# One-bank PSUM tiles and first conditioning rows from products in a hyperbolic transformer block

## The chip, the core and the metric

The kernel runs on one core of one Trainium2 chip. Its engines are TensorE (PE, matrix products; "PEld" is its weight load), VectorE (DVE), ScalarE (ACT), GpSimd (POOL) and SyncE (SP), which here issues all DMAs from one queue (SPq). The metric is the device time of one execution in microseconds (us). Three runs of the kernel before took 961.23, 961.72 and 963.40 us, so the median is 961.72. One more execution was profiled; it took 956.23 us, of which the span from first to last instruction is 954.2 us.

## What is computed

The input `x` is 128 sequences of 64 positions with 256 features, `cond` is one row of 256 features per sequence. A transformer block in hyperbolic coordinates runs on it, with six conditioning vectors per sequence (shift, scale and gate, for attention and for the MLP):

```python
ada = t_emb @ w_ada + b_ada
sh_msa, sc_msa, g_msa, sh_mlp, sc_mlp, g_mlp = jnp.split(ada, 6, axis=-1)
residual = x
xm = expmap0(layer_norm(logmap0(x)) * (1 + sc_msa) + sh_msa)
q, k, v = (_to_heads(plin(xm, w, b)) for w, b in ((w_q, b_q), (w_k, b_k), (w_v, b_v)))
qt, kt, vt = logmap0(q), logmap0(k), logmap0(v)          # 16 heads of 16
attn = jax.nn.softmax(einsum(qt, kt) / 4)
out_h = expmap0(einsum(attn, vt))
attn_out = plin(_from_heads(out_h), w_o, b_o)
x = mobius_add(residual, expmap0(g_msa * logmap0(attn_out)))
residual = x
xm = expmap0(layer_norm(logmap0(x)) * (1 + sc_mlp) + sh_mlp)
ff = plin(plin(xm, w_f1, b_f1), w_f2, b_f2)
return x_in + mobius_add(residual, expmap0(g_mlp * logmap0(ff)))
```

`expmap0` and `logmap0` scale a row by a function of its norm, and `plin` is a linear layer between them. The kernel folds most of these scalings into per-row factors, and folds the two MLP weights into one matrix `wm`, made once at the start.

## The kernel before

A tile is 128 partitions, which are two sequences of 64 positions. Four tiles (512 rows) are a quad, two tiles a pair; there are 16 quads and 32 pairs. The quads go through the block in groups: [0], [1,2], [3,4], ... [13,14], [15]. For each group the kernel does the attention of its quads (`attention`, with `attention_pair` for each pair), then the scalars of the Möbius addition (`scalars`, `inner`), then the MLP (`mlp`), and later the last addition and the store (`final`).

**The order is planned.** The Python code does not issue instructions. It records operations in `Plan.add`, each with the engines that may do it, a cost guessed by a formula and a key (the quad's number plus an offset for the kind of step from the table `pl.off`). `Plan.run` then plays the program through with five engines and chooses, whenever an engine is free, the ready operation with the lowest key for which buffers are free. `issue` emits the instructions in that order, and on the chip each engine runs its own list in order. So a change of a cost, a buffer count or an offset can move every instruction. `pl.hold` lets an engine wait a little for a better operation.

**Keep-warm products.** Where the plan finds PE with nothing to do and the share of busy time in the last 2.6 us below `share`, it puts in a 128x128 product of the identity with itself (`warm`, line 1394). Its result is read by nobody.

**PSUM.** The eight banks are four tensors of two banks. An operation asks for a "bank" or a "dbl", two neighbouring banks; class `Banks` hands them out. Three kinds of work use a double bank: the Q and K products of a pair (`qk`), whose squares are taken by one ACT instruction of 128x1024; the scores (`sc`), whose exponentials are two such instructions per pair; and attention times V (`av`), after which one reciprocal (line 505) and one product (`z`, line 483) of 128x512 normalise the heads.

**Conditioning.** At the start, `cond` is transposed and multiplied by `w_ada` in three slices of 512 columns; the bias `b_ada` is loaded as three broadcasts to all 128 partitions and added on DVE. The results are written to DRAM (`ada_d`), and `rows` reads them back for each quad so that each sequence's row stands on its 64 partitions. In `modulated`, DVE multiplies the normalised row by (1 + scale) (the tiles `mda`, `mdm`) and POOL (for quad 0 DVE or POOL) adds the shift (line 486). Quad 0 takes this way too: it waits for the first slice to be written and read back.

**Loads.** SP's queue takes cond, the first slice of `w_ada`, quad 0 of x, the bias, then the Q, K and V weights and biases. The rest of `w_ada` comes behind quad 0's first rows. `load_rest` loads the weights of the output projection and of the MLP once the gate rows are written, and makes `wm`. In `final`, the original x is loaded again (`xr`), POOL adds it (line 486, tile `x`), DVE does the last step (`p`), and a quad is stored by one DMA of 512 KB.

The lines named in profiles are those of helpers: 460 and 483 (`ts`, `tt` on DVE), 486 (`tt` on POOL), 494 (`stt`), 505, 509 (reciprocal, reduce), 519 and 521 (copy on DVE, ACT), 537 (ACT), 552 (products), 559 (transposes), 565 and 570 (DMA). Names without numbers are tile tags.

Of the kernel before, what the change touches and what calls it, by code (L numbers as in the profile page):

```python
# [66 lines left out]
class Buf:  # L67


    def __init__(self, ap, tag, bufs, space):  # L70
        self.ap, self.tag, self.bufs, self.space = ap, tag, bufs, space
        self.psum = space == "psum"
        self.n = {"dbl": 2, "bank": 1}.get(tag)
        self.log = []
        self.users = 0
        self.seq = self.place = None


class Banks:


    def __init__(self, pairs):
        self.pairs = pairs
        self.used, self.rel, self.n = [0] * 8, [k - 8 for k in range(8)], 0

    def place(self, k, n):
        return self.pairs[k // 2] if n == 2 else self.pairs[k // 2][:, 512 * (k % 2) : 512 * (k % 2) + 512]

    def room(self, pairs, single):
        n = [self.used[k] + self.used[k + 1] for k in range(0, 8, 2)]  # L90
        free = n.count(0)
        return pairs <= free and single <= n.count(1) + 2 * (free - pairs)

    def take(self, n):
        if n == 2:
            k = min((k for k in range(0, 8, 2) if not self.used[k] + self.used[k + 1]), key=lambda k: (max(self.rel[k : k + 2]), k))
        else:
            k = min((k for k in range(8) if not self.used[k]), key=lambda k: (-self.used[k ^ 1], self.rel[k], k))
        for i in range(k, k + n):
            self.used[i] = 1  # L100
        return k

    def give(self, k, n):
        for i in range(k, k + n):
            self.n += 1
            self.used[i], self.rel[i] = 0, self.n
# [6 lines left out]
class Plan:  # L113
# [3 lines left out]
    def __init__(self, nc, tc):  # L117
        self.nc, self.tc = nc, tc
        self.ops, self.byname, self.tags = [], {}, {}
        self.key, self.st, self.off = 0, "", {}  # L120

        self.early, self.late = 3, 13
        self.hold = {}

        self.span_, self.share, self.fill_occ = 2.6, 0.93, 0.22
        self.filler, self.fill = None, (0.0, 0.0)
        self.open = None
        self.pattern, self.sizes, self.places = None, {}, {}
# [21 lines left out]
    def allocate(self):  # L150

        for tag, (pool, n, bufs) in self.sizes.items():
            if tag == "bank":
                continue
            if tag == "dbl":
                self.banks = Banks([pool.tile([128, n], F32, tag=f"ps_{k}", name=f"ps_{k}", bufs=1) for k in range(bufs)])
                continue
# [5 lines left out]
    def real(self, ap):  # L163
# [7 lines left out]
        return bass.AP(place.tensor, int(place.offset) + p * full + at, [[full, dims[0][1]]] + dims[1:])  # L171

    def region(self, ap):
# [11 lines left out]
        return b, p0, p0 + dims[0][1], lo, hi  # L185
# [59 lines left out]
    def run(self):  # L245
# [3 lines left out]
        left = {}  # L249
# [33 lines left out]
        banks = self.banks  # L283

        def room(o):
            need = [0, 0, 0]
            for b in o.bufs:
                if b in started:
                    continue
                if b.psum:  # L290
                    need[b.n] += 1
                elif b.tag[0] == "j":
# [4 lines left out]
            return banks.room(need[2], need[1])  # L297

        while done < len(ops):
            progress = False  # L300
            for e in engines:
# [27 lines left out]
                if pick is None:  # L329
                    if e == "PE" and self.fill[0] < now < self.fill[1] and banks.room(0, 1):  # L330
# [8 lines left out]
                        o.place = banks.take(1)  # L339
                        o.eng, o.fn, o.occ, o.start, o.bufs, o.key = e, None, self.fill_occ, now, [], (-1, 0)  # L340
                        o.fn = lambda place=banks.place(o.place, 1): self.filler(place)
# [22 lines left out]
                for b in o.bufs:  # L364
                    if b not in started:
                        started.add(b)
                        if b.psum:
                            b.at = banks.take(b.n)
                            b.place = banks.place(b.at, b.n)
                            continue  # L370
# [32 lines left out]
            while events and events[0][0] <= now + 1e-9:  # L403
                _, _, kind, o = heapq.heappop(events)
                if kind:
                    if kind == 2:
                        banks.give(o.place, 1)
                    continue
# [5 lines left out]
                for b in o.bufs:  # L414
                    left[b] -= 1
                    if not left[b] and b.psum:
                        banks.give(b.at, b.n)
                    elif not left[b]:
# [122 lines left out]
    def mm(self, out, lhsT, rhs, start, stop, onto=False):  # L541
# [4 lines left out]
        elif k == 64:  # L546
            occ = 0.031
        elif k <= 4:
# [29 lines left out]
def kernel(  # L578
# [64 lines left out]
        "<": 3.13, "ada": 8.08, "ada<": 8.91, "ada>": 2.63, "adm": 6.68, "adm<": 0.86, "adm>": 3.73, "av": 6.27,  # L643
        "av<": 6.19, "av>": 9, "bx": 3.75, "bx<": 8.35, "bx>": 3.23, "by": 1.72, "by<": 7.27, "by>": 2.51,
        "bz": 8.84, "bz<": 9, "bz>": 8.09, "ch": 1.2, "ch<": 3.12, "ch>": 5.74, "ex": -2.28, "ex<": -1.01,
        "ex>": -2.07, "fya": 0.9, "fya<": -1.8, "fya>": -3.41, "fym": -0.66, "fym<": 0.44, "fym>": -3.06,
        "ga": 0.79, "ga<": 4.18, "ga>": 0.94, "gm": 7.6, "gm<": 6.4, "gm>": 4.08, "hc": -2.34, "hc<": -1.77,
        "hc>": 2.83, "hm": 0.09, "hm<": -1.26, "hm>": 8.38, "hmb": 4.87, "hmb<": 4.58, "hmb>": 3.29, "hw": 8.6,
        "hw<": 6.78, "hw>": 5.72, "hwb": -4, "hwb<": -0.68, "hwb>": 3.2, "kT": -3.99, "kT<": -2.26, "kT>": 7.07,
        "lx": 9, "lx>": 3.17, "mda": -3.73, "mda<": 6.71, "mda>": 2.67, "mdm": 3.44, "mdm<": 3.01, "mdm>": 3.8,  # L650
        "moa": 0.09, "moa<": -3.74, "moa>": 6.19, "mom>": 4.6, "mua": -3.27, "mua<": 8.51, "mua>": 4.6,
        "mum": 5.08, "mum<": -3.98, "mum>": 3.13, "n1": 7.39, "n1<": 7.97, "n2": 1.05, "n2<": -1.65, "n2>": -4,
        "nh": 1.09, "nh<": -3.36, "nh>": -0.28, "pga": -2.31, "pga<": 8.53, "pga>": 8.18, "pgm": 4.91,
        "pgm<": 2.12, "pgm>": 1.51, "qkb": -3.27, "qkb<": -1.57, "qkb>": 3.82, "qkv": 9, "qkv<": 1.92,
        "qkv>": 6.12, "qx": 3.05, "qx<": -3.07, "qx>": 7.2, "rTa": -3.91, "rTa<": -3.14, "rTa>": 5.83,
        "rTh<": 3.67, "rTh>": 0.63, "rTm": -0.86, "rTm<": 2.9, "rTm>": -2.04, "re": 0.52, "re<": -2.11,
        "re>": -2.61, "sc": 1.18, "sc<": -1.46, "sc>": 5.38, "sq": 0.11, "sq<": 5.18, "sq>": 3.43, "sua": -0.37,
        "sua<": 7.36, "sua>": -0.72, "sum": 4.1, "sum<": -1.33, "sum>": 8.02, "tpa": 2.48, "tpa<": 3.09,
        "tpa>": -4, "tpm": -0.56, "tpm<": 4.86, "tpm>": -3.52, "tq": 6.77, "tq<": 4.87, "tq>": 7.82,
        "tz": -1.39, "tz<": 3.93, "tz>": 1.94, "us": -1.51, "us<": 0.46, "us>": 4.29, "ve": -3.97, "ve<": 0.26,  # L660
        "ve>": 5.46, "wm<": 8.02, "wp": 1.64, "wp<": -4, "wp>": 4.46, "x1": 5.15, "x1<": -2.37, "x1>": -0.94,
        "xr": 7.25, "xr<": 5.99, "xr>": -1.89, "xsa": 3.1, "xsa<": -2.4, "xsa>": 2.48, "xsm": 8.6, "xsm<": 9,
        "xsm>": 8.95, "yTa": -1.74, "yTa<": -3.96, "yTa>": -1.77, "yTm": 7.78, "yTm<": -3.37, "yTm>": 8.19,
        "yya": 6.71, "yya<": -3.67, "yya>": -0.48, "yym": 5.91, "yym<": 5.07, "yym>": 4.92, "z": -2.23, "z<": 9,
        "z>": 1.15, "zT": 0.4, "zT<": -0.93, "zT>": 5.34,
# [13 lines left out]

    def dbl(name):  # L680
        return pl.tile(ps, [P, 1024], "dbl", name, 4, space="psum")
# [170 lines left out]

    cond_sb = T([P, D], "z", "cond_sb", 1)
    pl.dma(cond_sb, cond, 128 * KB)

    wada, bada, ada, behind = [], [], [], []
# [5 lines left out]
    wada.append([T([P, 1024], "yTm", f"wada1{c}", 2) for c in range(2)])  # L862
    bada += pair_of("bada0", "x1", 6)
    (ada0, ada1), (bada_, ada_) = pair_of("ada0", "x1", 6), pair_of("bada2", "x1", 6)
    bada.append(bada_)
    ada += [ada0, ada1, ada_]
    for c in range(2):
        pl.dma(wada[0][c], w_ada[c * P : (c + 1) * P, 0:512], 256 * KB)
    load_x(0)
    pl.dma(bada[0], b_ada[0:512].partition_broadcast(P), 256 * KB)  # L870
# [16 lines left out]
    pl.dmas(  # L887
        [
            (bqkv[p : p + 1, c * D : (c + 1) * D], b.unsqueeze(0))
            for p, c, b in ((0, 0, b_q), (0, 1, b_k), (33, 0, b_q), (33, 1, b_k), (64, 0, b_v), (65, 1, b_v))  # L890
        ],
        6 * KB,
    )
    for c in range(2):
        behind.append(pl.dma(wada[1][c], w_ada[c * P : (c + 1) * P, 512 : 6 * D], 512 * KB))
    for n in (1, 2):
        behind.append(pl.dma(bada[n], b_ada[n * 512 : (n + 1) * 512].partition_broadcast(P), 256 * KB))

# [10 lines left out]
    for n in range(3):  # L909
        aps = bank(f"aps{n}")  # L910
        with pl.group("PE"):
            for c in range(2):
                w = wada[0][c] if n == 0 else wada[1][c][:, (n - 1) * 512 : n * 512]
                pl.mm(aps, condT[:, c, :], w, c == 0, c == 1)
        for h in range(2):
            k = 2 * n + h
            part = slice(h * D, (h + 1) * D)
            one = 1.0 if k in (1, 4) else 0.0
            pl.stt(ada[n][:, part], aps[:, part], one, bada[n][:, part], ALU.add, ALU.add)
            if k in (1, 2, 4, 5):  # L920
                k0 = k - 1 if k in (1, 4) else k
                lo = max(0, k0 - 2 * n) * D
                if k in (1, 2, 5):
                    wrote = pl.dma(parts[k0], ada[n][:, lo : (h + 1) * D], (k - k0 + 1) * 128 * KB)
                else:
                    pl.dma(parts[3][:, 0:D], ada[1][:, D : 2 * D], 128 * KB)
                    pl.dma(parts[3][:, D : 2 * D], ada[2][:, 0:D], 128 * KB)

    def load_rest():
# [567 lines left out]
```

## Time and profile before

| | |
|---|---|
| median of 3 runs | 961.72 us |
| profiled execution / its span | 956.23 / 954.2 us |
| mean granted PE clock | 0.905 |
| real products and transposes / keep-warm products in the program | 4769 / 331 |
| bytes moved by DMA | 90.44 MB, 95 GB/s over the span |
| quad 0: first QKV product starts | 24.2 us |
| quad 0: last MLP product ends | 177.6 us |
| last attention product ends | 864.6 us |
| last MLP product of the last quad ends | 931.9 us |

A product in float32 is two passes on PE, a transpose one, and the profile counts passes. A row of the groups reads: line, engine, operation, output tile and inputs, shape, count, then busy us in all and mean ns of one, then the idle time of the engine just before and what ended it. "PEclk" is the clock that PE was granted in each of 40 slices, in tenths. Windows give, for a stretch of the span, the busy time of each engine with the number of instructions in brackets.

### The profile page before, as it was taken

The page shows a single profiled execution, that of the slowest core. Times are in us where ns is not written, and L with a number is a line of the kernel's source. Part 1 is how long each engine was busy: PE and PEld are TensorE (multiplying, and loading weights), DVE is VectorE, ACT ScalarE, POOL GpSimd, SP SyncE. Part 2 cuts the span into 40 slices and gives each one's busy share as a digit, 9 for nine tenths or more (in the row PEclk, how much of TensorE's full clock was granted, in tenths as well). Part 3 has the DMA queues.
Part 4 walks back from the last instruction along what each step waited for, and adds up shares of the span by engine and source line. Part 5 has one row for each costly group of instructions (what it writes and reads, how often), then busy time and mean ns, then how long its engine had stood idle before and what let it go on. Part 6 is the DMA issues. An engine that isn't in the chain of part 4 may idle for free. (4 is left out here: it accounts for less than half of the span.)

```text
span 954.2 us, 24232 instructions
## 1 busy us (share of the span) xinstructions
PE 822.7 (86%) x9334; PEld 582.5 (61%) x9334; DVE 680.8 (71%) x2781; ACT 501.0 (53%) x1482; POOL 123.7 (13%) x100
## 2 busy tenths in 40 slices
PE   7889898998888888888888888888888798787988
PEld 6465555565665675665665666666655575466777
DVE  5668876788846876678764887678755876568964
ACT  2255753467554584456635575465634654355452
POOL 0011200012100121013200221001400221011111
PEclk9989997999998898979898899979979979779989
DMA  7675562324311362115511163114621223113212
GB/s 227 173 222 143 137 140 58 90 68 138 96 36 34 90 175 71 34 36 147 153 45 46 56 189 100 35 35 135 160 50 44 79 79 90 30 39 100 67 55 90
DMA packets 75743, 90.44 MB, mean 95 GB/s; under 512 B 7270, under 2 KB 57708, under 8 KB 75628
## 3 DMA queue, kind: packets, MB, share of 16 engines
q1 hardware_dynamic: 75628, 88.90, 33.8%
q8 instruction: 73, 1.20, 0.5%
q14 instruction: 42, 0.34, 0.1%
HBM read 79.70 MB, written 9.18 MB: 93 GB/s over the span
## 5 line engine op out<-in xcount | busy, mean ns | idle before, releaser
L552 PE MATMUL ps<-wqkv,yTa 128*128 128x512 f32 (+1 forms) x512 | 198.5, 537 | 3.2 <-ACT ja L537 1.0
L552 PEld LDWEIGHTS ps<-wqkv,yTa 128*128 128x128 f32 x512 | 102.8, 210 | 89.1 <-issue 68.6
L552 PE MATMUL ps<-wm,yTm 128*128 128x256 f32 (+1 forms) x512 | 123.9, 400 | 14.2 <-DVE jd L494 2.2
L1394 PE MATMUL ps<-ident 128*128 128x128 f32 x662 | 104.0, 312 | 33.2 <-ACT pt L537 9.6
L552 PEld LDWEIGHTS ps<-wm,yTm 128*128 128x128 f32 x512 | 99.8, 217 | 42.5 <-ACT rTm L521 4.7
L1394 PEld LDWEIGHTS ps<-ident 128*128 128x128 f32 x662 | 92.8, 219 | 47.1 <-ACT pt L537 10.5
L486 POOL TENSOR_TENSOR x<-x,xr 128x512 f32<-128x512 f32 x32 | 41.1, 1302 | 484.2 <-ACT x L537 461.4
L552 PEld LDWEIGHTS ps<-ve,pt 64*64 64x64 f32 x4096 | 72.8, 152 | 10.8 <-issue 5.4
L552 PE MATMUL ps<-ve,pt 64*64 64x17 f32 x4096 | 76.2, 219 | 0.9 <-issue 0.6
L537 ACT ACTIVATE pt<-ps 128x1024 f32<-128x1024 f32 x64 | 61.9, 1019 | 19.8 <-PE ps L552 19.5
L486 POOL TENSOR_TENSOR ya<-ya,mda 128x512 f32<-128x512 f32 x30 | 39.9, 1334 | 201.0 <-ACT p L521 67.1
L552 PE MATMUL ps<-wo,zT 128*128 128x256 f32 x256 | 61.2, 381 | 0.2
L494 DVE SCALAR_TENSOR_TENSOR p<-ps,fh,gm 128x256 f32<-128x256 f32 x64 | 28.7, 479 | 43.9 <-PE ps L552 17.8
L486 POOL TENSOR_TENSOR ym<-ym,mdm 128x512 f32<-128x512 f32 x32 | 42.0, 1316 | 137.4 <-DVE ym L483 78.5
L537 ACT ACTIVATE qx<-ps,par 128x512 f32<-128x512 f32 x64 | 42.7, 684 | 30.8 <-PE ps L552 18.0
L559 PE MATMUL ps<-ident,u 128*128 128x128 f32 x256 | 43.4, 314 | 8.9 <-ACT pt L537 3.4
L537 ACT ACTIVATE ja<-ps,fh 128x256 f32<-128x256 f32 x64 | 30.3, 473 | 36.9 <-PE ps L552 16.2
L552 PEld LDWEIGHTS ps<-wo,zT 128*128 128x128 f32 x256 | 45.9, 190 | 6.1 <-DVE zT L519 1.2
L552 PE MATMUL ps<-qx,kT 32*64 32x128 f32 x2048 | 45.1, 307 | 4.8 <-DVE kT L519 1.2
L552 PE MATMUL ps<-bqkv,rTa 2*128 2x512 f32 x192 | 46.5, 676 | 3.1 <-ACT rTa L521 1.4
L494 DVE SCALAR_TENSOR_TENSOR jd<-ps,ym 128x256 f32<-128x256 f32 x64 | 27.1, 423 | 27.4 <-PE ps L552 23.3
L552 PEld LDWEIGHTS ps<-qx,kT 32*64 32x64 f32 x2048 | 35.4, 145 | 17.2 <-issue 7.7
(274 smaller groups left out, 1535.1 us busy)
## 6 DMA issues: line engine op xcount, KB each, us to landing
mda<-ada_d SPq DMA_DIRECT2D x64, 256.0 KB, 4.3
mdm<-ada_d SPq DMA_DIRECT2D x64, 256.0 KB, 5.0
x<-in_x_dram SPq DMA_DIRECT2D x16, 512.0 KB, 7.0
xr<-in_x_dram SPq DMA_DIRECT2D x32, 256.0 KB, 4.9
ga<-ada_d SPq DMA_DIRECT2D x64, 128.0 KB, 3.1
gm<-ada_d SPq DMA_DIRECT2D x64, 128.0 KB, 3.0
out_dram<-p SPq DMA_DIRECT2D x16, 512.0 KB, 3.9
xp<-in_x_dram SPq DMA_DIRECT2D x26, 256.0 KB, 2.8
```

Of the source, the lines that this page charges most:

```text
L486: fn2 = lambda: self.nc.gpsimd.tensor_tensor(R(out), R(a), R(b), op)
L494: fn = lambda: self.nc.vector.scalar_tensor_tensor(R(out), R(a), R(s), R(b), op0, op1, **({} if accum is None else {"accum_out": R(accum)}))
L537: fn = lambda: self.nc.scalar.activation(R(out), R(a), func, scale=R(scale), **{k: R(v) for k, v in kw.items()})
L552: fn = lambda: self.nc.tensor.matmul(R(out), lhsT=R(lhsT), rhs=R(rhs), start=start, stop=stop, skip_group_check=onto)
L559: fn = lambda: self.nc.tensor.matmul(R(out), lhsT=R(a), rhs=ident, start=start, stop=True, is_transpose=True, skip_group_check=not start)
L1394: nc.tensor.matmul(place[:, 0:P], lhsT=ident, rhs=ident, start=True, stop=True)
```

## The change

It has six parts.

1. **PSUM**: eight tensors of one bank, handed out in turn; `Banks` and `dbl` are gone. Squares of Q and K are two ACT instructions of 128x512 per pair instead of one of 128x1024, exponentials four instead of two, reciprocal and normalisation two each (128x16 and 128x256) instead of one.
2. **First rows from products**: for quad 0 and attention only, the rows of shift and scale are made in PSUM by products. A repeated `cond` (`crep`, 64 columns per sequence) times the first slice of `w_ada`, onto a one-row product that puts in the bias. DVE then does (scale + 1) times the row and adds the shift, straight from PSUM.
3. **Bias of the conditioning** by a one-row product too, from one loaded row instead of 128.
4. **Loads**: quad 0 of x first, then cond, four rows of bias, the first slice of `w_ada`, the Q, K, V weights; in `load_rest` the MLP weights first, then the projection's, then the other slices of `w_ada`, with the two later conditioning products recorded after them. The `xr` loads wait for the MLP of their own quad (`then`) instead of an early row.
5. **The end**: for the last quad the addition of `xr` may go to DVE, and the store is two DMAs of 256 KB. The shift of the conditioning goes to POOL alone up to the third last quad, and to DVE or POOL after that.
6. **The plan's numbers**: `pl.off` has other values throughout, `share` is 0.92 for 0.93, PE's and DVE's `hold` 0.41 and 0.06 for 0.22 and 0.03.

```diff
-        qk = dbl(f"qk{tag}").rearrange("p (t n) -> p t n", t=2)
+        qk = [bank(f"qk{t}{tag}") for t in range(2)]
...
-        pl.act(usq, qk, AF.Square)
+        for t in range(2):
+            pl.act(usq[:, t], qk[t], AF.Square)
...
-        for k in range(2):
+        for k in range(4):
             pl.act(
-                pt[:, 2 * k : 2 * k + 2].rearrange("p r t f e s -> p (r t f e s)"),
-                sc[k].rearrange("p r t f n -> p (r t f n)"), AF.Exp, scale=GC * GC / math.sqrt(HD),
+                pt[:, k].rearrange("p t f e s -> p (t f e s)"), sc[k].rearrange("p t f n -> p (t f n)"),
+                AF.Exp, scale=GC * GC / math.sqrt(HD),
             )
...
-        pl.recip(rd, ah[:, :, :, HD : HD + 1])
-        pl.tt(
-            z.rearrange("p b t h d -> p b (t h) d"), ah[:, :, :, 0:HD], rd.to_broadcast([P, 2, 16, HD]), ALU.mult
-        )
+        for b in range(2):
+            ah = av[b].rearrange("p (h e) -> p h e", h=16)
+            pl.recip(rd[:, b], ah[:, :, HD : HD + 1])
+            pl.tt(
+                z[:, b].rearrange("p t h d -> p (t h) d"), ah[:, :, 0:HD], rd[:, b].to_broadcast([P, 16, HD]), ALU.mult
+            )
...
+    crep = T([P, 2, 8, S], "qx", "crep", 1)
+    pl.copy(crep, condT[:, :, 0:8].unsqueeze(3).to_broadcast([P, 2, 8, S]))
+    conditioning(0)
+    pl.st = "md"
+    first = [bank(f"md{t}") for t in range(4)]
+    with pl.group("PE"):
+        for t in range(4):
+            pl.mm(first[t], onesP[32 * t : 32 * t + 1, :], bada[0][32 * t : 32 * t + 1, :], True, False)
+    for t in range(4):
+        with pl.group("PE"):
+            for c in range(2):
+                pl.mm(
+                    first[t], crep[:, c, 2 * t : 2 * t + 2, :].rearrange("p e s -> p (e s)"), wada[0][c], False, c == 1
+                )
...
+        for t in range(4 if i0 == k0 == 0 else 0):
+            pl.st = "mu" + tag[0]
+            pl.stt(y[:, t, :], first[t][:, D : 2 * D], 1.0, y[:, t, :], ALU.add, ALU.mult)
+            pl.tt(y[:, t, :], y[:, t, :], first[t][:, 0:D], ALU.add)
...
+                last = quads[-1] == NQ - 1
+                pl.tt(x1[:, t - 1 : t + 1, :], x1[:, t - 1 : t + 1, :], xr, ALU.add, eng="DVE/POOL" if last else "POOL")
...
+                if last:
+                    pl.dma(out_t[:, i0 + t - 1 : i0 + t + 1, :], p2[:, t - 1 : t + 1, :], 256 * KB)
...
-    pl.hold = {"PE": (0.22, 9999.0), "DVE": (0.03, 60.0)}
+    pl.hold = {"PE": (0.41, 9999.0), "DVE": (0.06, 60.0)}
```

In the built programs this gives 4784 real products for 4769 and 271 keep-warm products for 331, ACT 96 more instructions for squares and exponentials, DVE 64 more for reciprocals and normalisation, and four DMAs of 256 KB fewer for the rows.

## The prediction

> **What bounds the kernel now.** I read the engine totals first, then the rate by slices, then the same split by stage, then the keep-warm products alone.
>
> ```profile
> PE 822.7 (86%) x9334; PEld 582.5 (61%) x9334; DVE 680.8 (71%) x2781; ACT 501.0 (53%) x1482; POOL 123.7 (13%) x100
> ...
> PEclk9989997999998898979898899979979979779989
> DMA  7675562324311362115511163114621223113212
> ```
>
> PE leads, but 104 of its 822.7 us are the products of line 1394, which compute nothing. Real work is 718.7 us, 75% of the span; no engine is full. A planned, fixed order with short waits on ACT and DVE bounds it, and only the start (DMA row: 7) leans on DMA. Cut at the first QKV product, the end of quad 0's MLP products and the end of the last attention products:
>
> ```profile
> 0.00:24.20 24.20, 18.10 (x121) 14.98 (x121) 13.89 (x59) 6.62 (x20) 0.70 (x6) 1.00 0.74 229
> 24.20:177.60 153.40, 137.97 (x1630) 88.31 (x1628) 113.02 (x478) 72.56 (x199) 13.71 (x10) 0.94 0.56 144
> 177.60:864.60 687.00, 590.55 (x7103) 414.34 (x7101) 489.09 (x1909) 382.36 (x1120) 93.88 (x72) 0.89 0.29 81
> 864.60:954.20 89.60, 76.12 (x491) 64.89 (x487) 64.78 (x336) 39.49 (x143) 15.44 (x12) 0.94 0.27 77
> ```
>
> Columns: stretch and length, then busy us of PE, weight loads, DVE, ACT, POOL, granted clock, DMA share, GB/s. The keep-warm products alone (PE, weight loads, clock, DMA):
>
> ```profile
> 0.00:24.20 24.20, 12.93 (x106) 12.77 (x106) 1.00 0.74 229
> 24.20:177.60 153.40, 5.97 (x26) 5.01 (x24) 0.94 0.56 144
> 177.60:864.60 687.00, 40.36 (x215) 33.41 (x215) 0.89 0.29 81
> 864.60:931.90 67.30, 25.63 (x169) 23.26 (x169) 0.95 0.28 78
> 931.90:954.20 22.30, 19.12 (x150) 18.36 (x150) 0.92 0.23 75
> ```
>
> Each is recorded as two passes. They fill the start and the end; in the middle they are a symptom of gaps of the plan.
>
> **Part by part.** My sum is an identity for PE: span = work + keep-warm + idle, stretch by stretch. The built order of both kernels gives the number of keep-warm products: up to the end of quad 0's MLP 65 before and 4 after; then to the last attention product 107 and 74; then to the last MLP product 84 and 94; behind it 75 and 99. Together 331 and 271.
>
> *Start, to 24.2 us.* What ends the wait here is not the conditioning's way through DRAM: DVE stood only 0.7 us for the loaded rows of line 486's tile. The chain is x's load (landed 7.82), its statistics (8.9 us on DVE and ACT, to 16.72), modulation, transposes. After, x is first in SP's queue: 512 KB ahead of cond's 128 KB. Cond landed 2.2 us after its issue; 384 KB more at 229 GB/s is 1.7, so x lands near 4.7 instead of 7.82, and the chain with two DVE steps put in (a 1024-wide copy, some 1.1, and two at 0.42) ends near 15.5. But the first rows now come from products: eight of 128x512, 16 passes at 0.457 (six passes of the wm stage took 2.74) = 7.3, plus seven one-row bias products, 14 passes at the bqkv row's 0.24 or, four of them side by side, some 2.9. They need wada0, behind x and cond: 1.16 MB, landing near 7.3. The four row biases can run before that; then come the conditioning product (four passes, 1.8, and a bias 0.5) and the eight: 9.6 us, the first of them cold (the first four such passes took 3.78 instead of 1.83), so to about 19. The last row's two DVE steps (0.84) and transposes and copies as before (21.53 to 24.20, 2.7) give the first QKV product near 22.5, **-1.7**. The 10.2 us of new PE work take the place of 50 keep-warm products (12.2 us). Bounds: -4 (all PE work warm) to +2 (wada0 late). SP's queue: x's next three quads and w1 go past the q/k/v biases, which then land near 30; they are needed after eleven us of QKV products for both pairs, at 33, so covered. Two xr loads (0.5 MB at 21.62 us) go behind the start.
>
> *24.2 to 177.6.* Keep-warm 12 to 1, and w1's transposes and wm's products fill in: at 5.97/13 = 0.46 each, **-5.4** (0 to -8; three broadcast biases and four row loads gone are 1.75 MB, 7.7 us of DMA at 229 GB/s, which ends a wait only where a load is late).
>
> *Middle.* 33 fewer keep-warm products at 40.36/107.5 = 0.375: -12.4. Against it stand the split operations:
>
> ```profile
> L537 ACT ACTIVATE pt<-ps 128x1024 f32<-128x1024 f32 x64 | 61.9, 1019 | 19.8 <-PE ps L552 19.5
> L537 ACT ACTIVATE usq<-ps 128x1024 f32<-128x1024 f32 x32 | 32.5, 1017 | 24.6 <-PE ps L552 24.6
> L537 ACT ACTIVATE vsq<-ps 128x512 f32<-128x512 f32 x32 | 19.0, 594 | 32.2 <-PE ps L552 29.8 <-DVE fim L460 1.1 <-DVE kT L519 1.0
> ```
>
> A two-bank step costs 1.02, a one-bank step 0.594. Exponentials: 4 x 0.594 - 2 x 1.019 = 0.34 a pair; squares 2 x 0.594 - 1.017 = 0.17. On DVE 128x256 from PSUM takes 0.418 (x<-ps,ga): 2 x 0.418 - 0.683 = 0.15 for z; a 128x16 reciprocal isn't in the trace: between 128x8 (0.20) and 128x32 (0.349), about 0.25, so 0.15 more. Together 0.81 a pair, 25.9 us over 32 pairs. How much shows? In the chain of waits after 733 us, with six pairs, stand one of six squares, three of twelve exponentials and two and a half of six z steps: 0.03 + 0.085 + 0.125 = 0.24 a pair, 7.6 in all. Bounds 0 and 25.9. I take **-12.4 + 7.6 = -4.8**. The Trainium skill (Advanced Engine Details and Errata, The Read-Write Bubble) speaks against this part: each ACT or DVE instruction shows its memory latency anew, and one instruction may read several banks. Its table in VectorE: DVE Perf Modes gives 172 cycles fixed on ACT's 1.2 GHz, an estimated 0.143 a split and 13.8 us for 96 splits; the rows give 0.17 and 16.4. Either is hidden except where the chain goes through it, so I keep the rows.
>
> Fewer keep-warm products may cool PE. The skill's rule (TensorE: Matmul & The Clock Gate, What's actually happening) is that half clock comes after a whole idle window of some 3.4 us. The trace:
>
> ```profile
> 280.00:284.00 4.00, 2.15 (x11) 1.59 (x12) 1.65 (x6) 1.89 (x7) 0.00 (x0) 1.00 0.38 131
> 284.00:288.00 4.00, 4.00 (x128) 3.24 (x130) 2.04 (x7) 3.07 (x13) 0.00 (x0) 0.63 0.04 9
> 288.00:292.00 4.00, 4.00 (x18) 2.23 (x15) 0.00 (x0) 0.41 (x2) 0.00 (x0) 0.52 0.20 63
> ```
>
> Here 1.85 us idle in four brought 6.8 us at half clock ((0.37 + 0.48) x 4 / 0.5), while PE was full of 64x17 products. By the rule the removal is free; by the row a half-idle stretch does it, and each costs 3.4 us of passes. Mean clock 0.905 means 181 us, some 27 such stretches. I take no change in their number, as gaps shrink too.
>
> *End.* Before: 159 keep-warm products in 44.75 us (0.281 each), 31.4 us of work, 13.5 idle. After: 193 at 0.281 = 54.3 + 31.4 = 85.7 if idle vanishes (-3.9), 99.2 if it stays (+9.6). The order groups the last three MLPs and leaves their final steps (12 x 0.42 on ACT, 5 x 1.30 on POOL, 12 x 0.50 on DVE) behind them. The end itself:
>
> ```profile
> SPq L1493 <- DMA out_dram<-p: 2.6, 1, 2.6
> SPq L1493 <- PE ps L1394: 1.9, 1, 1.9
> ```
>
> After the last output landed the program still waited 1.9 us for keep-warm products. So halving that output and giving one add to DVE (0.7 for 1.3) saves nothing as long as 99 of them stand at the end. Ninety-nine at 19.12/75 = 0.255 are 25.2 for 19.1: I take **+5.0**.
>
> **Sum:** -1.7 - 5.4 - 4.8 + 5.0 = -6.9. The profiled execution took 956.23 (span 954.2 and 2.0 around it), so 949.3. The median shown is 961.72, 5.5 above that execution; with the same step: **954.8**. The eight one-bank tiles, the removed pair allocator and the pauses allowed to the planner act only through this order.
>
> **Rivals.**
> - *Splits exposed* (slower). Every pair's chain usq, reciprocal, exponentials, z is serial, and ACT's waits on PE (24.6 + 19.5 us above) say it sits behind PE. If all 25.9 shows: -6.9 + 18.3 = +11.4, 973.1. It turns slower once 14.5 of the 25.9 is exposed. Against: ACT is at 53%.
> - *Cooler PE* (slower). Five more half-clock stretches: +17.0 - 6.9 = +10.1, 971.8; two even the sum out.
> - *The start's gain goes through* and the end stays: -1.7 - 8.0 - 4.8 + 0 = -14.5, 947.2. For: DMA share 0.74 and 0.56. Against: the end has more keep-warm products.
> - *The order doesn't do what it counts*: gaps return as waits, 961.7.
>
> **Chances.** Forecast 0.36, splits exposed 0.22, cooler PE 0.14, gain goes through 0.19, nothing 0.09. Under 0.2% (1.9 us) either way can't be told from no change; faster 0.52, same 0.11, slower 0.37. All lower bounds together give -28, all upper ones +25; I cut to 942 to 975. The forecast's own range is 949 to 961.
>
> **What would show it.** Right: first QKV product near 22.5; quad 0's MLP products end near 170; 542 keep-warm passes near 85 us; ACT busy near 518; the clock within 0.01 of 0.905; the tail behind the last MLP product 27. Wrong: PE idle in the middle above its 96 us by more than 10; mean clock under 0.89; a QKV product waiting for a bias or for w1.

## The result and the profile after

Four runs of the changed kernel took 790.22 to 792.59 us, median 792.12, beside 962.56 for the kernel before in the same session. The ratio is **0.821** [0.816, 0.826]. I had forecast 954.8 with a range of 942 to 975. Direction right, size wrong by 163 us, which is far outside the range. The times here are medians of all executions; the ratios compare means without the slow executions, those over 1.5% above their kernel's fastest.

The engine totals, the granted clock and the DMA share of the changed kernel:

```profile
span 790.8 us, 24161 instructions
...
PE 738.0 (93%) x9244; PEld 525.5 (66%) x9244; DVE 682.3 (86%) x2842; ACT 502.9 (64%) x1588; POOL 123.5 (16%) x98
...
PEclk9999899999999999999999999998999998999999
DMA  5938436411651157214731364213641225113314
```

DVE and ACT do what they did before (680.8 and 501.0 us then). PE is 84.7 us less busy and 78.7 us less idle (52.8 for 131.5), and its mean clock is 0.976 for 0.905. The same stretches as in the prediction, in the order length, then busy PE, weight loads, DVE, ACT, POOL, clock, DMA share, GB/s:

```profile
0.00:21.90 21.90, 16.21 (x46) 7.01 (x46) 14.08 (x63) 6.23 (x19) 0.70 (x6) 1.00 0.62 204
21.90:166.60 144.70, 138.74 (x1634) 88.47 (x1632) 123.18 (x544) 76.66 (x237) 13.00 (x10) 0.95 0.54 148
166.60:704.00 537.40, 504.84 (x7019) 361.66 (x7020) 471.11 (x1883) 376.48 (x1184) 90.80 (x68) 0.98 0.37 102
704.00:765.90 61.90, 56.27 (x358) 46.86 (x358) 53.60 (x267) 33.51 (x118) 12.19 (x9) 0.97 0.31 86
765.90:790.80 24.90, 21.92 (x194) 21.53 (x192) 20.37 (x89) 10.00 (x32) 6.78 (x5) 1.00 0.34 106
```

| stretch | before | after | difference | my step |
|---|---|---|---|---|
| to the first QKV product | 24.2 | 21.9 | -2.3 | -1.7 |
| to the end of quad 0's MLP | 153.4 | 144.7 | -8.7 | -5.4 |
| to the last attention product | 687.0 | 537.4 | **-149.6** | **-4.8** |
| the end | 89.6 | 86.8 | -2.8 | +5.0 |

So 150 of 163 us lie in the middle, where the change has nothing but the split operations, the tensors, another order and later `xr` loads. There PE idles 32.6 us instead of 96.5, and its keep-warm products take 27.3 us instead of 40.4:

```profile
166.60:704.00 537.40, 27.33 (x152) 22.55 (x152) 0.98 0.37 102
```

Real products take 477.5 us (504.84 - 27.33) instead of 550.2 (590.55 - 40.36). The clock alone, 0.89 to 0.98, would make about 500 of the 550, an estimate.

**What the stall is.** In the prediction I showed the row of `vsq`, the squares of V, with "29.8 <-PE ps L552" as the idle time before it, and used only its duration. One of these waits in the kernel before, in the timeline (start, us, engine, line, operation; in brackets the idle time before it and who ended it):

```profile
370.59 1.02 ACT L537 ACTIVATE usq<-ps 128x1024 f32<-128x1024 f32 x1 [0.43 <-PE ps L552]
...
372.37 4.77 PEld L552 LDWEIGHTS ps<-wm,yTm 128*128 128x128 f32 x15 [1.50 <-issue]
372.38 5.01 PE L552 MATMUL ps<-wm,yTm 128*128 128x256 f32 x14
375.34 0.60 ACT L537 ACTIVATE vsq<-ps 128x512 f32<-128x512 f32 x1 [3.73 <-PE ps L552]
375.97 0.69 DVE L509 TENSOR_REDUCE hs<-vsq 128x32 f32<-128x512 f32 x1 [2.99 <-ACT vsq L537]
```

The pair's QKV products end near 372.4. ACT is free from 371.61. But `vsq` starts at 375.34, in the middle of MLP products that it doesn't read, and DVE stands idle for 2.99 us until it has `vsq` for the sum `hs`. In the built program, the PE instruction whose count this `vsq` waits for is a `wm,yTm` product into columns 384 to 511 of the tensor `ps_2`; `vsq` reads columns 512 to 1023 of the same tensor, which is the other bank. In these programs a wait is placed per tensor, so two banks with unrelated work wait for each other. I counted such waits in the built programs (both instructions touch the same PSUM tensor, no common bank and no common data elsewhere): **518 in the kernel before, none in the changed one**. The waits run in both directions: ACT for PE 112, PE for ACT 108, DVE for PE 101, PE for DVE 79, the rest between ACT and DVE. In the changed kernel's trace no idle time stands before any of the 32 `vsq`, and nobody waits for them (both lists are empty):

```profile
L492 ACT ACTIVATE vsq<-bank x32: 575/605/659, 36.4 to 666.4; 128x512 f32<-128x512 f32 x32
its engine sat idle before it (us, times) until:
who waited for it (us, times):
```

That is a theory with a count; whether the count makes the time is for the runs.

### The profile page after: what moved, and what is told of

Its sections match the earlier page's. It is cut to its first block, busy times and chain, and to the rows that moved or that the text cites. A ratio compares the mean times of both kernels' runs of the same rounds, so it can differ in the third digit from the quotient of the medians.

```text
span 790.8 us, 24161 instructions
## 1 busy us (share of the span) xinstructions
PE 738.0 (93%) x9244; PEld 525.5 (66%) x9244; DVE 682.3 (86%) x2842; ACT 502.9 (64%) x1588; POOL 123.5 (16%) x98
## 4 chain that ended last, share of the span: by engine, by line
DVE 43%; PE 35%; ACT 8%; DMA 7%; issue 4%; SPq 1%; POOL 1%; DVEq 0%; ACTq 0%; POOLq 0%
PE bank L509 25%; PE bank L516 6%; ACT ja L492 5%; DVE jd L449 4%; DVE x L449 4%; PE bank L1373 4%; DMA mdm<-ada_d 3%; DVE hs L464 3%; DVE u L438 3%; DMA xp<-in_x_dram 2%; DVE p L449 2%; DVE ve L438 1%; DVE z L438 1%; DVE mxq L438 1%; DVE ym L438 1%
## 5 line engine op out<-in xcount | busy, mean ns | idle before, releaser
L509 PE MATMUL bank<-wqkv,yTa 128*128 128x512 f32 (+1 forms) x512 | 175.4, 490 | 3.2 <-DVE yTm L474 3.2
L509 PEld LDWEIGHTS bank<-wqkv,yTa 128*128 128x128 f32 x512 | 93.9, 190 | 73.9 <-issue 63.8
L509 PE MATMUL bank<-wm,yTm 128*128 128x256 f32 (+1 forms) x512 | 106.8, 362 | 0.5 <-DVE rTh L474 0.4
L509 PEld LDWEIGHTS bank<-wm,yTm 128*128 128x128 f32 x512 | 89.6, 195 | 17.1 <-issue 2.3
L441 POOL TENSOR_TENSOR x<-x,xr 128x512 f32<-128x512 f32 x31 | 40.4, 1314 | 339.1 <-ACT x L492 326.7
L1373 PE MATMUL bank<-ident 128*128 128x128 f32 x542 | 75.3, 291 | 5.2 <-ACT ja L492 3.7
L1373 PEld LDWEIGHTS bank<-ident 128*128 128x128 f32 x542 | 69.1, 202 | 10.3 <-ACT ja L492 4.0
L492 ACT ACTIVATE pt<-bank 128x512 f32<-128x512 f32 x128 | 67.3, 604 | 10.3 <-PE bank L509 10.2
L509 PEld LDWEIGHTS bank<-ve,pt 64*64 64x64 f32 x4096 | 63.3, 135 | 11.4 <-issue 3.7
L509 PE MATMUL bank<-ve,pt 64*64 64x17 f32 x4096 | 66.7, 208 | 1.0 <-issue 0.9
L509 PE MATMUL bank<-wo,zT 128*128 128x256 f32 x256 | 61.2, 381 | 0.4 <-issue 0.3
L492 ACT ACTIVATE qx<-bank,par 128x512 f32<-128x512 f32 x64 | 43.1, 688 | 13.8 <-PE bank L516 13.8
L516 PEld LDWEIGHTS bank<-ident,u 128*128 128x128 f32 x256 | 30.4, 149 | 22.5 <-ACT pt L492 12.9
L492 ACT ACTIVATE usq<-bank 128x512 f32<-128x512 f32 x64 | 35.4, 596 | 12.1 <-PE bank L509 11.7
```

The lines of the kernel that those rows point to most:

```text
L441: fn2 = lambda: self.nc.gpsimd.tensor_tensor(R(out), R(a), R(b), op)
L492: fn = lambda: self.nc.scalar.activation(R(out), R(a), func, scale=R(scale), **{k: R(v) for k, v in kw.items()})
L509: fn = lambda: self.nc.tensor.matmul(R(out), lhsT=R(lhsT), rhs=R(rhs), start=start, stop=stop, skip_group_check=onto)
L516: fn = lambda: self.nc.tensor.matmul(R(out), lhsT=R(a), rhs=ident, start=start, stop=True, is_transpose=True, skip_group_check=not start)
L1373: nc.tensor.matmul(place[:, 0:P], lhsT=ident, rhs=ident, start=True, stop=True)
```

## The experiments

The rival to "separate tensors" was that the new plan (order, splits, first rows, loads) makes the gain, and that the tensors only come with it. Times are medians; each ratio is against the kernel before on the same chip (957.94 us in the first session, 961.75 in the second, 958.54 in the third; these lie within 0.5% of each other). The plan's model doesn't know of these extra waits, so putting banks into common tensors leaves the recorded order as it is.

**1. The changed kernel, its banks laid as halves of four two-bank tensors.**

```diff
...
         for tag, (pool, n, bufs) in self.sizes.items():
+            if tag == "bank":
+                pairs = [pool.tile([128, 1024], F32, tag=f"bank_{k}", name=f"bank_{k}", bufs=1) for k in range(4)]
+                self.places[tag] = collections.deque(p[:, 512 * h : 512 * h + 512] for p in pairs for h in range(2))
+                continue
```

> The changed kernel with its order kept to the instruction; only the eight banks are the halves of four tensors of two banks, as in the kernel before. In the built program 670 waits then name an instruction that touches only the other bank of the same tensor (0 in the changed kernel, 518 in the one before). Theory 'shared tensor': these waits are what cost the 163 us; the time goes back most of the way, to 900-1000, PE idle rises from 53 us to over 110 and the clock falls under 0.93. Rival 'plan' (the order, the first rows and the loads are the gain): 792 give or take 8, PE idle 50-60.

Measured: **937.43 us**, ratio 0.978 [0.972, 0.985], with 670 waits on the other half. Its totals and clock:

```profile
PE 811.4 (87%) x9244; PEld 561.8 (60%) x9244; DVE 685.2 (73%) x2842; ACT 506.5 (54%) x1588; POOL 124.1 (13%) x98
...
PEclk9999988998999899998799998979998688898999
```

The same instructions on each engine in the same order as in the 792 us kernel, and 145 us of the gain are gone. PE is idle for 122.5 us (933.9 - 811.4) at a clock of 0.921, all as the theory had it.

**2. The kernel before in its own order, with eight tensors.** A two-bank operation is emitted as two.

```diff
-self.banks = Banks([pool.tile([128, n], F32, tag=f"ps_{k}", name=f"ps_{k}", bufs=1) for k in range(bufs)])
+self.banks = Banks([pool.tile([128, 512], F32, tag=f"ps_{k}", name=f"ps_{k}", bufs=1) for k in range(2 * bufs)])
...
+    def emitted(self, fns):
+        (e, _, occ, lat, lock), = self.ops[-1].ways
+        self.ops[-1].ways = [(e, lambda: [f() for f in fns], occ, lat, lock)]
...
         pl.act(usq, qk, AF.Square)
...
+        real = pl.real
+        pl.emitted([lambda t=t: nc.scalar.activation(real(usq[:, t]), real(qk[:, t]), AF.Square, scale=1.0) for t in range(2)])
```

(The exponentials, the reciprocal and `z` likewise.)

> The kernel before with its order kept; its eight banks are eight tensors, and each two-bank instruction is emitted as two one-bank ones in the same place (96 more on ACT, 64 more on DVE, which are 16 and 10 us busy). 'Shared tensor': 800-850, PE idle under 80, clock over 0.95. 'Plan': 960-985, as the added instructions cost and nothing is gained.

Measured: **796.07 us**, ratio 0.831 [0.826, 0.837], 4 us below the theory's interval, no such wait left. Its totals and clock:

```profile
PE 744.7 (94%) x9334; PEld 536.7 (67%) x9334; DVE 680.3 (86%) x2845; ACT 502.2 (63%) x1578; POOL 125.3 (16%) x100
...
PEclk9999999899999999999989999999999989999999
```

The old order, with the old first rows, loads and table, has nearly the whole gain. The intervals of this ratio and of the changed kernel's just touch, so what all the rest is worth together is about 1% and not resolved.

**3. The same, but with the halves of two-bank tensors**: splits without separation.

```diff
+halves = [pool.tile([128, n], F32, tag=f"ps_{k}", name=f"ps_{k}", bufs=1) for k in range(bufs)]
+self.banks = Banks([t[:, 512 * h : 512 * h + 512] for t in halves for h in range(2)])
```

> As the run before, the same split instructions, but on halves of four two-bank tensors; 715 waits on the other bank. 'Shared tensor': no gain, 960-1010. Second rival 'two-bank instructions' (one instruction over two banks holds both until its end, and splitting it sets them free earlier): as fast as the run with eight tensors, 800-850.

Measured: 961.43 us, ratio 1.0038 [1.0005, 1.0070], 715 waits. Splitting costs 0.4%, some 3.6 us, with the 197 further waits that come with it, and brings nothing. Runs 2 and 3 differ in the tensors alone: 165 us.

**4. Only two of eight banks share a tensor** (changed kernel).

```diff
+            if tag == "bank":
+                pair = pool.tile([128, 1024], F32, tag="bank_p", name="bank_p", bufs=1)
+                alone = [pool.tile([128, 512], F32, tag=f"bank_{k}", name=f"bank_{k}", bufs=1) for k in range(6)]
+                self.places[tag] = collections.deque([pair[:, 0:512], pair[:, 512:1024]] + alone)
+                continue
```

> The changed kernel in its own order, with two of its eight banks laid in one two-bank tensor and the other six in tensors of their own: 187 waits in the built program are for an instruction of the other half of the pair, against 0 with eight tensors and 670 with four pairs. Theory (each such wait costs, wherever it falls): a share of 187/670 of the 145 us that lie between eight tensors (792.1 us) and four pairs (937.4 us), so near 792 + 40 = 832 us, 815 to 850, and clock near 0.96. Rival (the loss comes only when most banks are coupled and TensorE cools; one pair is covered by the other six banks): 790 to 800 us at a clock above 0.97.

Measured: **826.47 us**, ratio 0.861 [0.855, 0.868]. The time is the theory's (832), the clock of 0.975 the rival's. One pair costs 34 us:

```profile
PE 750.5 (91%) x9244; PEld 527.7 (64%) x9244; DVE 682.9 (83%) x2842; ACT 504.4 (61%) x1588; POOL 125.1 (15%) x98
...
PEclk9999899999999999999999999999999799999999
```

PE's idle time is 73.6 us for 52.8, at a mean clock of 0.975 for 0.976. So the wait costs by itself, before the clock falls; with four pairs the clock falls too (0.921). PE is also 12.5 us longer busy (750.5 for 738.0) at the same clock, and why is open.

**5. Other halves: banks k and k+4 of the rotation in one tensor.**

```diff
...
+                self.places[tag] = collections.deque(p[:, 512 * h : 512 * h + 512] for h in range(2) for p in pairs)
...
```

> The changed kernel in its own order on four two-bank tensors, as the earlier run with pairs of neighbours (937.4 us), but with banks k and k+4 of the rotation as the two halves, so that the other half is usually the bank of another, older or much younger, operation. In the built program 658 waits still name an instruction of the other half (670 with neighbours). Theory (such a wait costs because its two halves are in use at the same time by unrelated work, whatever their distance in the rotation): 900 to 960 us at a clock below 0.94. Rival (only neighbours hurt, since their products follow each other at once; far halves are long done when they are waited for): 790 to 850 us. The result also tells whether a mere other numbering of the banks would have done the work of eight tensors.

Measured: **961.09 us**, ratio 1.0001 [0.9962, 1.0040]; 1 us above the theory's interval, and the rival is out. The whole gain of 170 us is gone, with the changed kernel's order, splits, first rows and loads all in place. Its profiled execution (span 965.5, one of the three longest of ten):

```profile
PE 824.7 (85%) x9244; PEld 567.3 (59%) x9244; DVE 684.4 (71%) x2842; ACT 507.2 (53%) x1588; POOL 124.2 (13%) x98
```

These are close to the kernel before's totals (822.7, 680.8, 501.0). This numbering of banks is no substitute for separate tensors; others were not tried. Three rows of the waits, first in the changed kernel, then here (who waited and for whom; us in all, times, longest):

```profile
ACT pt L492 <- PE bank L509: 10.2, 7, 3.0
DVE hs L464 <- ACT usq L492: 5.7, 2, 3.9
DVE rd L460 <- PE bank L509: 7.2, 11, 2.1
...
ACT pt L496 <- PE bank L513: 31.9, 18, 6.0
DVE hs L468 <- ACT usq L496: 25.9, 11, 4.0
DVE rd L464 <- PE bank L513: 21.8, 12, 4.2
```

`vsq`, the example above, waits for PE only 2.9 us here and 7.3 us in run 1: the loss sits in other rows than in the kernel before, and no single row prices it. Nor does the count: 518 such waits go with 162 us (the kernel before and run 2), 658 with 170 us and 670 with 145 us. So it may be luck that the share 187/670 came near in run 4. Why far halves are worse than neighbours is open; it may be that neighbours are often taken by the same step. The 20 us that run 1 keeps against the kernel before are therefore not the worth of the rest of the change.

**6. No keep-warm products at all** (they feed nothing, so the output is the same).

```diff
-                o.fn()
+                if o.key != (-1, 0):
+                    o.fn()
```

> The changed kernel without any of its keep-warm products; nothing else is moved. The profile of the changed kernel has 75.3 us of them and 52.8 us of idle TensorE. Theory (the clock stays up because TensorE no longer waits at the shared tensors; keep-warm products fill what is left and some of them are in the way): clock 0.95 to 0.98 and 785 to 800 us. Rival (the clock of 0.976 is bought with the keep-warm products, and the gain of the change rests on them): clock below 0.93, PE busy on real products up by 30 us or more, 815 us or longer.

Measured: 804.12 us, ratio 0.838 [0.833, 0.844]. Both expectations missed in part: the clock did fall to 0.917 and real products take 695.3 us, 32.6 more than in the changed kernel (738.0 - 75.3 = 662.7), as the rival said; but the time rose by 12 us only, as 75.3 us of keep-warm products are gone. The clock by slices:

```profile
PEclk9998999997999979999999999997999879985895
```

It falls most at the end, where the kernel runs out of real products: to 0.73 behind 704 us, and to 0.94 for 0.98 between 166.6 and 704. So 12 us is what the keep-warm products are worth in this order, out of 170.

**7. Quad 0's first rows through DRAM as before** (changed kernel; planned anew).

```diff
...
-        for t in range(4 if i0 == k0 == 0 else 0):
+        for t in range(0):
...
-        for h in range(0 if i0 == k0 == 0 else 2):
+        for h in range(2):
```

> The changed kernel with the first rows of conditioning of quad 0 taken by the way that the other quads take (two products on the row, through DRAM and back on all partitions) in place of the four products per row tensor. It shows the worth of that part. My prediction had 1.7 us at the first product of QKV and 5.4 us up to the end of quad 0. Theory: 2 to 8 us longer than the changed kernel, so 794 to 800 us, with the first product of QKV near 24. Rival (the start is hidden or the new products cost what they save): 788 to 793 us.

Measured: 823.69 us, ratio 0.860 [0.853, 0.867], outside both expectations. Part of it is at the start, in the timeline:

```profile
13.51 0.34 SPq L527 DMA_DIRECT2D ada_d<-x  x1
13.90 1.59 SPq L527 DMA_DIRECT2D x<-in_x_dram  x3
15.53 1.18 SPq L527 DMA_DIRECT2D xp<-in_x_dram  x2
...
16.81 2.61 SPq L527 DMA_DIRECT2D mda<-ada_d  x4
...
32.62 1.88 PE L509 MATMUL bank<-wqkv,yTa 128*128 128x512 f32 x5
```

The write of the rows (`ada_d`) is issued at 13.51 and their load (`mda`) at 16.81, behind five loads of x; in the kernel before these stood at 10.65 and 12.71. The first QKV product starts at 32.62 instead of 21.93, and quad 0's last MLP product at 192.0 instead of 166.0. The last quad's starts 28 us late (792.4 for 764.6), so nearly all of the loss has happened by quad 0's end; the 15 us of it that come between the first QKV product and there are not explained. The clock is as good (0.977); the plan put in 798 keep-warm passes for 542, 108.2 us for 75.3. The run suggests that the changed loads need the changed first rows; it doesn't show what the first rows are worth in the old kernel: run 2 keeps DRAM rows and the old load order, and has its first QKV product at 22.9.

**8. The changed kernel with the table, share and pauses of before.**

```diff
-    pl.hold = {"PE": (0.41, 9999.0), "DVE": (0.06, 60.0)}
+    pl.hold = {"PE": (0.22, 9999.0), "DVE": (0.03, 60.0)}
```

(`share` and `pl.off` likewise.)

> The changed kernel with the table of offsets, the share and the pauses of the kernel before; the eight tensors, the split operations and the first rows stay. It shows the worth of the new table. The kernel before with eight tensors took 796.1 us with that table. Theory (separate tensors carry the gain, the table is worth little): 788 to 805 us. Rival (the table is fitted to the changed kernel and carries tens of us of the gain): 815 us or longer.

Measured: 829.02 us, ratio 0.866 [0.858, 0.873]: the rival's side, against my theory. Yet run 2 had the same table at 796. So the old numbers cost 37 us on the changed kernel, and planned an order for the kernel before that needs only 796. They seem to fit the kernel for which they were set. Runs 7 and 8 therefore don't price their part, since each is a new plan; the two differences can't be added, and their sum (68 us) is far above the 4 us between the medians of run 2 and the changed kernel.

**9. Without the keep-warm products behind the last real product.**

```diff
-            for o in self.order:
-                o.fn()
+            last = max(n for n, o in enumerate(self.order) if o.eng == "PE" and o.key != (-1, 0))
+            for n, o in enumerate(self.order):
+                if n < last or o.key != (-1, 0):
+                    o.fn()
```

> The changed kernel without the 97-99 keep-warm products behind the last real product. My prediction held that they outlast the last store and set the end by 1.9 us. If that holds in the changed kernel too: 2-4 us less. If the store ends last (its trace shows a wait for the store and none for PE at the end): 792 within 1.5.

Measured: 789.14 us, ratio 0.826 [0.820, 0.833]: 3.0 us less, as my prediction's step would have it, but its own four executions reach from 788.01 to 797.54. So both once more, side by side, six executions each:

> The changed kernel as it is, once more, on the same chip and in the same rounds as the one without keep-warm products behind the last real product. Theory (those products lie beside the tail's DVE work and the output's DMA, and the end is not theirs): the two within 3 us of each other, 787 to 795 us. Rival (my prediction's step, 5 us for keep-warm products that delay the end): the changed kernel 4 us or more longer than the one without.

> The changed kernel without the keep-warm products behind the last real product, in the same rounds as the changed kernel itself. Theory: within 3 us of it, 786 to 793 us. Rival: 4 us or more shorter.

Measured: the changed kernel 790.62 us (787.63 to 795.14), ratio 0.824 [0.820, 0.828]; without those products 793.30 (788.50 to 802.26), ratio 0.826 [0.822, 0.831]. The same within the noise. In both the program's end waits for the output and for no keep-warm product; first the changed kernel's wait of SP's queue, then the other's:

```profile
SPq L1474 <- DMA out_dram<-p: 1.6, 2, 0.9
SPq L1476 <- DMA out_dram<-p: 1.6, 2, 0.9
```

No run beats the changed kernel clear of noise.

## Why the prediction was wrong

**The step that failed** is the last sentence of the sum: "The eight one-bank tiles, the removed pair allocator and the pauses allowed to the planner act only through this order." Runs 1, 4 and 5 keep the order and change nothing but which banks share a tensor (run 5 with the banks renumbered): 937, 826 and 961 us for 792. Run 2 keeps the old order and separates the banks: 796. The tensors act directly, and they are the change. I priced each edit by instructions, shapes and queue places, and an edit that adds and removes no instruction got no price. What it removed were waits, and I never asked whether the instruction that ended a wait had made what was waited for. That the direction came out right is luck: the -6.9 us came from other terms, and what all of these are worth is about 1% and not resolved (run 2).

The evidence was in a row I quoted: 29.8 us of ACT waiting for PE ahead of `vsq`. I read such waits as "short waits on ACT and DVE" of a fixed order. The timeline around one of them (above) has the product finished, the reader idle and another stage's product running.

Point by point:

- *Start, -1.7*: right, and for its reasons. -2.3; first QKV product at 21.93, forecast near 22.5. PE has 10.2 us more real work and 12.1 us less of keep-warm products, forecast 10.2 and 12.2.
- *24.2 to 177.6, -5.4*: -8.7, just beyond the bound of -8; quad 0's MLP products end at 166.6, forecast near 170. The keep-warm term was right (-5.3); beside it stand 6.1 us more real work and 9.5 us less idle time, which the sum had at nothing.
- *Middle, -12.4 + 7.6 = -4.8*: -149.6. The keep-warm term was right (-13.0 for -12.4). The split term was of the right order: 3.6 us in run 3, further waits included, for 7.6. What was absent is idle time, -63.9, and the time of real products, -72.7, most of it the clock by the estimate above.
- *Splits on ACT*: I forecast ACT busy near 518, it is 502.9. The rows of exponentials and squares rose by 8.3 us together (67.3 + 35.4 against 61.9 + 32.5), not by 16.4: a one-bank exponential lasts 604 ns in the record but takes 67.3/128 = 526 ns of ACT's time, since successive ones overlap in the record. Adding means over instructions overstated the price; the other estimate, 13.8, did so too. Other rows of ACT fell by 6.4 us.
- *Clock within 0.01 of 0.905*: wrong, 0.976. I had taken half-clock stretches as fixed in number, some 27. The traces grant either the full or the half clock: half for 35 stretches, 181 us together, in the kernel before, and for 8, 37.5 us, in the changed one. They went with the stalls. The rule that I weighed (the Trainium skill, TensorE: Matmul & The Clock Gate, What's actually happening: half clock after a whole idle window, some 3.4 us) doesn't fit the kernel before, and there the measurement decides: no gap of PE between two products is as long, as far as their modelled ends tell. The longest is 3.1 us (`PE ps L1394 <- ACT pt L537: 9.6, 4, 3.1`). How much idle time it takes stays open: run 4 has 40% more PE idle time at the same clock, run 6 twice the idle time at 0.917.
- *End, +5.0*: wrong in sign, -2.8. Idle time fell by 4.9 us, and the keep-warm products of the end took 1.8 us more, not 9.6, at 0.242 each for 0.281. The tail is 24.9 us, forecast 27, and DVE works in 20.37 of them. The last output's DMA ends the program, not PE; the two kernels of experiment 9 show that the keep-warm products there cost nothing that can be measured. The step let the 99 keep-warm products set the end; its own figures differ by 6.1 us, and the 5.0 taken has no working.
- *Rivals*: splits exposed and a cooler PE both fell. No rival let a tensor's boundary cost time.

Over the whole span the 163 us can be split by an estimate from the two traces. PE was busy for 173.3 us in half-clock stretches before and for 36.1 after; if half of that is lost, the clock makes 69 us, idle time 79 and fewer keep-warm products 17, and the real products' work is the same within 2 us. That the stalls bring the half clock is inferred from the two going together in runs 1, 2, 3 and 5; in run 4 the idle time rose alone.

## What to carry to other kernels

Before pricing a change of tiles, ask in the trace of waits whether the instruction that ends a wait touches the same data, and if it doesn't, what it shares: here the two-bank tensors made 518 such waits, and without them the same order took 162 us less. Give each PSUM bank that is filled and drained on its own a tensor of its own; one shared pair out of four already cost 34 us. To price one part of a kernel whose order is planned, change it in a way that keeps the order, since planning anew with numbers set for another kernel cost 37 us in run 8.

## What was not expected of the hardware

Two banks of PSUM that one engine writes and another reads at the same time showed no sign of disturbing each other in these totals. Run 1 and the changed kernel have the same instructions in the same order, the one with waits between the banks of a tensor and the other without; without them DVE is busy for 682.3 us against 685.2 and ACT for 502.9 against 506.5. The stalls were in the program's waits. And the clock needed far less filling here than I had thought once PE had its work in time: with no keep-warm product at all the mean clock was 0.917, above the 0.905 that the kernel before reached with 104 us of them.
